# First addition of a layer's terms by an accumulating transfer, the last pairs' layer 2 apart, and quarter sums taken in an earlier sweep

## Chip, cores and metric

One core of one Trainium2 chip. The metric is device time in microseconds (us), the median of repeated executions of one program; lower is better. One further execution of the same program was taken with the hardware profiler.

## What is computed

Eight batches of a graph with 2048 nodes and 64 features go through four layers, each `x = layernorm(x + layer(x))`, all in fp32:

```python
# layer 0: Chebyshev terms of the adjacency A, weights made per node from an embedding of 16
As = [I, A, 2 A A - I]
x_g = einsum('knm,bmc->bnkc', As, x)
w   = einsum('nd,dkio->nkio', embedding, weight)
y   = einsum('bnki,nkio->bno', x_g, w) + einsum('nd,do->no', embedding, bias)
# layer 1: attention; e[i,j] = leaky_relu(s1[i] + s2[j]), masked by A > 0.5, softmax over j
y   = elu(einsum('bij,bjc->bic', softmax(where(A > 0.5, e, -9e15)), x))
# layer 2: (A + I) @ (x W^T + b) / rowsum(A + I)
# layer 3: node 0 set to given values, then three times
effects = einsum('nm,bmd->bnd', A, v)
v = relu([v, effects] @ W1^T + b1) @ W2^T + b2
```

A is 2048 x 2048, 16 MB, and does not stay on the chip: every product with it streams it again from device memory.

## The kernel before

Two batches make a pair, 128 columns, so there are four pairs (0 to 3). A product with A is a sweep: A comes as 32 tiles of 256 rows by 512 columns (512 KB each), and each tile feeds two fp32 matmuls of 128x512 per product (line 1094). Six buffers (`a_ring`) hold A tiles, and SyncE's queue (SP) fetches them in order (`fetch`, line 234). A sweep can serve two products from the same tiles.

Layer 0 needs two products with A for each pair. The first sweep serves pairs 0 and 1 (and also makes the layer 1 masks); the second product of a pair shares a sweep with the first product of a later pair, and the second product of pair 3 has a sweep of its own. After the two products come the per-node weights (`second_pass`, line 576): for each of 16 row tiles of a pair, 16 terms of 128x128 are made, one for each embedding element. PE makes eight at a time in `yp` (line 601), and `add_terms` (line 613) lets ScalarE (ACT) scale them by the embedding into a `terms` buffer of 1 MB, one of four in `e_ring` (line 624). For pairs 1 to 3 all 16 terms are stored; for pair 0 VectorE (DVE) folds the second eight onto the first eight (line 627), so eight are left. Line 636 then adds up the 16 (or 8) terms by one strided `tensor_reduce` into `added`, and line 639 adds `added` to the rows of the pair in `SX`.

Layer 1 (`layer1`, line 660) runs per pair and works mostly on DVE: `scores` finds each row's greatest score with 32 passes of 2048 elements (line 732), which need row masks loaded by GpSimd's queue (POOL, line 719); `weights` makes the softmax weights, with two additions on DVE (lines 810 and 823) and two kinds of activations on ACT (lines 818 and 826) for each of 32 column tiles, in buffers of the same `e_ring`, and PE multiplies them with the rows (line 837). `finish` normalises. A pair's rows are ready for layer 2 when `("x2", p)` is set.

Layers 2 and 3 of pairs 0 and 1 are one sweep and three sweeps each. Pairs 2 and 3 are joint (`JOINT`). Their layer 3 uses a Strassen-Winograd form: seven products of half size in place of eight, for which sums of the quarters of A are needed (`s1` to `s4`, 32 tiles in device memory). Before, `joint_layer2` (line 1189) makes layer 2 of both pairs in one sweep, which starts when both pairs are ready. It takes the tiles by groups of four, one of each quarter (`quarters`, line 1132), and after each group `sums` (line 1160) makes four sum tiles on DVE (line 1173), each in a buffer of `bc_ring`, and POOL's queue stores them (line 1175). Layer 2 reads A + I, so tiles on the diagonal are fetched again without I (`pure`, line 1150, eight in all).

The order is not left to a scheduler. A `Plan` (line 38) simulates the kernel while it is written: work is cut into generators ("threads"), each of which says which engine its next step needs and after what; `go` takes the step that can begin first, ties going to the lower rank, and adds a cost from small formulas (`dve`, `act`, `mm`, `plan.dma`). Instructions are emitted in that order, each engine executes its own in order, and semaphores keep the data safe. So a cost that is wrong in the plan does no harm to the values, but the engine then meets its instructions at other times than planned. A transfer is planned as 0.7 us of issue on POOL (0.4 on SP), 3.5 us, its size at 340 GB/s, and 0.2 us. `SLACK` (line 46) is added to the time at which PE may take a step.

Of the kernel before, what the change touches and what calls it, by code (L numbers as in the profile page):

```python
# [37 lines left out]
class Plan:  # L38
# [7 lines left out]
    SLACK = 1.0  # L46
# [97 lines left out]
def resnorm_d4_kernel(  # L144
# [288 lines left out]
    def row_tile(t, an, k, done):  # L433
        yield "ACT", [done]
        dg = tiny([P, 1], "dg", 2)
        nc.scalar.activation(an, an, AF.Copy, accum_out=dg)
        done = plan.run("ACT", act(N) + 0.2, done)
        yield "DVE", [done, mr_ring]
        nc.vector.tensor_scalar_add(dg, dg, 1.0)
        nc.vector.reciprocal(rdeg[:, t : t + 1], dg)  # L440
        mk, km = mr_ring.take([P, N], "mr", BF16)
        nc.vector.tensor_scalar(mk, an, THRESHOLD, NEG_INF, ALU.is_le, ALU.mult)
        done = plan.run("DVE", 1.13 + 0.26, done)
        bc_ring.give(k, done)
        nc.gpsimd.dma_start(by_row[t], mk)
        done = plan.dma("DMA", 512, done)
        mr_ring.give(km, done)
        at["by_row", t] = done
        if all(("by_row", i) in at for i in range(NT)):
            at["rows"] = done  # L450
# [99 lines left out]

    def stacks():

        for n in range(NPAIR * NCH):
            p, c = n // NCH, n % NCH
            yield "DMA", [xg_ring, ("y1T", p, c)]
            xg, kx = xg_ring.take([P, 2, CW], "xgT")
            nc.gpsimd.dma_start(
                xg[C:P], y1_cols[p].rearrange("(e c) n -> c e n", c=C)[:, :, cols(c)]
            )
            got = plan.dma("DMA", 256, xg_ring.t, ("y1T", p, c))  # L560
            yield "PE", [pp_ring]
            pt, km = pp_ring.take([P, CW], "ps_xg")
            for j in range(TPC):
                nc.tensor.transpose(pt[:, j * P : (j + 1) * P], SX[p][:, c * TPC + j, :], ident)
            t_pe = plan.run("PE", tr(TPC), pp_ring.t)
            for e in range(2):
                eng = yield EITHER, [t_pe]
                copy(eng, xg[0:C, e, :], pt[e * C : (e + 1) * C])
                done = plan.run(eng, cost(eng, CW), t_pe)
            pp_ring.give(km, done)  # L570
            stacked.append((xg, kx))
            at["xg", len(stacked)] = max(done, got)
# [40 lines left out]
    def add_terms(p, c, t, h, yp, ring, k, terms, t_pe, left):  # L613
# [16 lines left out]
        if h == 0:  # L630
            at["terms", p, t] = done
            return
        yield "DVE", [done]
        n = 8 if shared else D0
        added = tiny([P, P], "added", 1)
        nc.vector.tensor_reduce(  # L636
            added, terms[0][:, 0:n, :].rearrange("p d n -> p n d"), AX.X, ALU.add
        )
        nc.vector.tensor_tensor(v, v, added, ALU.add)
        done = plan.run("DVE", dve(n * P) + dve(P) + 0.1, done)  # L640
# [19 lines left out]
    def layer1(p):  # L660
# [7 lines left out]
        for c in range(NCH):  # L668
# [30 lines left out]
        plan.start(10 + p, scores(p, sv, xc, s_rows, done))  # L699

    def scores(p, sv, xc, s_rows, done):
        s2b = []
        for e in range(2):
            yield "DMA", [bc_ring, done, "rows"]
# [238 lines left out]
    def z_evict(p, c, pa, give, done):  # L943
# [4 lines left out]
        give(done)  # L948
# [187 lines left out]
    def order_of_joint():  # L1136
        for k in range(2):
            for r in range(RQ):
                order_of_a.extend((c, q, True) for c, q in quarters(k, r))
# [10 lines left out]
    def pure(k, r):  # L1150

        yield "SP", [("group", k, r), *([xg_ring] if len(xg_ring.freed) > 1 else [NEVER])]
        got = []
        for c, q in (quarters(k, r)[i] for i in (0, 3)):
            t, kt = xg_ring.take([P, 2, CW], "pure")
            nc.sync.dma_start(t, tile_of_adj(c, q))
            got.append((t, kt, plan.dma("SP", 512, xg_ring.t)))
        return got

    def sums(k, r, taken):  # L1160

        tiles4 = [(t, kt, got) for t, kt, got, _ in taken]
        own = {}
        if r // 2 == k:
            own = dict(zip((0, 3), (yield from pure(k, r))))
        a11, a12, a21, a22 = ((own.get(i) or tiles4[i])[0] for i in range(4))
        ready = [(own.get(i) or tiles4[i])[2] for i in range(4)]

        def out_of(m, a, b, op, *after):
            yield "DVE", [bc_ring, *after]  # L1170
            t, kt = bc_ring.take([P, 2, HALF], m)
            t = t.rearrange("p a b -> p (a b)")[:, 0 : 2 * CW].rearrange("p (t n) -> p t n", n=CW)
            nc.vector.tensor_tensor(t, a, b, op)
            done = plan.run("DVE", dve(2 * CW), *after)
            nc.gpsimd.dma_start(sum_tiles[m][k, r], t)  # L1175
            bc_ring.give(kt, plan.dma("DMA", 512, done))
            return t, done

        s3, d3 = yield from out_of("s3", a11, a21, ALU.subtract, ready[0], ready[2])
        s1, d1 = yield from out_of("s1", a21, a22, ALU.add, ready[2], ready[3])  # L1180
        s2, d2 = yield from out_of("s2", s1, a11, ALU.subtract, d1)
        s4, d4 = yield from out_of("s4", a12, s2, ALU.subtract, d2)
        for (_, kt, _, free), d in zip(taken, (d2, d4, d1, d1)):
            a_ring.give(kt, max(free, d))
        for _, kt, _ in own.values():
            xg_ring.give(kt, d2)
        refill()

    def joint_layer2():
        p, o = JOINT  # L1190
        at["group", 0, 0] = 0.0
        for k in range(2):
            pas = {}
            for r in range(RQ):
                taken = []
                for i, (c, q) in enumerate(quarters(k, r)):
                    n = next(used)
                    if r == 0 and i in (0, 2):
                        if i == 0:
                            yield "PE", [po_ring, ("x2", p), ("x2", o)]  # L1200
                            t2, kp = po_ring.take([P, 2, CW], "po")
                            pas[c] = [(t2[:, e, :], kp) for e in range(2)]
                        else:
                            pas[c] = []
                            for e in range(2):
                                yield "PE", [acc_ring]
                                pas[c].append(acc_ring.take([P, CW], "acc"))
                    for e, pair in enumerate(JOINT):
                        yield "PE", [("a", n)]
                        t, kt = a_tiles[n]  # L1210
                        for b in range(2):
                            m = 2 * q + b
                            nc.tensor.matmul(
                                pas[c][e][0],
                                lhsT=SX[pair][:, m, :],
                                rhs=t[:, b, :],
                                start=(r == 0 and i in (0, 2) and b == 0),
                                stop=(r == RQ - 1 and i in (1, 3) and b == 1),
                            )
                        done = plan.run("PE", mm(CW, 2), ("a", n))  # L1220
                        if r == RQ - 1 and i in (1, 3):
                            if i == 3:
                                give = lambda t, kk=pas[c][e][1]: acc_ring.give(kk, t)
                            else:
                                give = give_half(pas[c][e][1])
                            plan.start(1, z_evict(pair, c, pas[c][e][0], give, done))
                    del a_tiles[n]
                    taken.append((t, kt, at["a", n], done))
                    if i == 0:
                        nxt = (k, r + 1) if r + 1 < RQ else (k + 1, 0)  # L1230
                        at[("group", *nxt)] = plan.free["PE"]
                    spent[0] += 1
                plan.start(5, sums(k, r, taken))
                refill()

    halves_left = {}

    def give_half(kp):
        def give(t):
            left, last = halves_left.pop(kp, (2, 0.0))  # L1240
            if left == 1:
                po_ring.give(kp, max(t, last))
            else:
                halves_left[kp] = (1, max(t, last))

        return give
# [142 lines left out]
    def layer2_product(p):  # L1389
        return product(  # L1390
            SX[p],
            lambda c, pa, ka, done: z_evict(p, c, pa, lambda t: acc_ring.give(ka, t), done),
# [12 lines left out]
    def sweeps():  # L1405

        order_of_a.extend((c, q, False) for _ in range(NPAIR) for c, q in sweep_of_a)
        for p in range(NPAIR - 2):
            for s in range(4):
# [4 lines left out]
        for p in range(NPAIR):  # L1414
            products = [second_product(p)]
            if 0 < p < NPAIR - 1:
                products.append(first_product(p + 1))
            yield from sweep(*products)
        for p in range(NPAIR - 2):
            yield from sweep(layer2_product(p))  # L1420
            for s in range(3):
                yield from sweep(layer3_product(p, s))

# [3 lines left out]
        yield from joint_layer2()  # L1427
# [51 lines left out]
```

## Time and profile before

| | |
|---|---|
| runs shown | 2167.12, 2170.16, 2171.02 us; median 2170.16 |
| profiled execution | 2166.21 us; span in the trace 2164.4 us |
| mean granted TensorE clock | 0.991 |
| busy: PE, DVE, ACT, POOL | 2081.7, 1552.5, 977.9, 213.6 us |
| moved by the DMA engines | 495.84 MB, 229 GB/s over the span |

Where the stages lie, by the first and last instruction of their lines: the weights of layer 0 (line 601) from 149 to 1020 us; the sweep for pair 3's second product from 778 to 932 us; the layer 1 scores (line 732) from 332 to 1506 us and weights (line 810) from 423 to 1657 us; the joint layer 2 from 1675 to 1815 us, with its sums on DVE from 1692 to 1827 us; the joint layer 3 from 1815 to 2153 us.

How to read it: PE's rows are modelled at their end, so the distance from one start to the next, and the time in which PE has nothing begun, say more than the mean of a row. The page's slices are 54 us each. "A <- B" in a list of waits reads: the engine stood still before A, and B ended the wait. Waits of an engine off the path cost nothing by themselves. "PEld" is the loading of weights into PE; its idle time "<- issue" is its normal pace.

### The profile page before, as it was taken

Reading aid. Unit: us, or ns where it says so; the run is one execution under the profiler, and the core shown is the slowest. Engines: PE = TensorE matmul, PEld = TensorE weight load, DVE = VectorE, ACT = ScalarE, POOL = GpSimd, SP = SyncE. Lnnn points to the kernel's source line nnn. Section 1 sums busy time; section 2 is a strip of 40 time slices with the busy share of each in tenths; the row PEclk is TensorE's granted clock in tenths of the full one; section 3 lists DMA queues with packets and bytes.
Section 4 is the critical chain, followed back from the end, with each engine's and each line's share of the span. In section 5 each row is a group of like instructions: output and inputs, shape, how many; then the busy total and the mean of one; then the engine's idle time right before and its main releaser. Section 6 shows DMA issues by size and latency. Waiting matters only on the chain.

```text
span 2164.4 us, 18851 instructions
## 1 busy us (share of the span) xinstructions
PE 2081.7 (96%) x6325; PEld 917.0 (42%) x6325; DVE 1552.5 (72%) x1727; ACT 977.9 (45%) x1799; POOL 213.6 (10%) x374
## 2 busy tenths in 40 slices
PE   8999999899999999999999999999999899999998
PEld 3444344334333343333444454443444344444444
DVE  2227648998899999879999979999697455020214
ACT  0025424367776556767653757516676022000002
POOL 2310000101010110110001011010010110000000
PEclk9999999999999999999999999999999999999999
DMA  9899835634353364543669778788776667878785
GB/s 300 268 335 345 290 105 197 218 102 127 90 170 125 116 211 160 180 156 122 232 239 371 232 250 323 250 320 300 247 252 234 231 249 271 283 249 283 252 290 187
DMA packets 208739, 495.84 MB, mean 229 GB/s; under 512 B 20275, under 2 KB 28595, under 8 KB 204531
## 3 DMA queue, kind: packets, MB, share of 16 engines
q1 hardware_dynamic: 165058, 347.62, 47.2%
q0 software_dynamic: 39360, 144.92, 19.6%
q10 hardware_dynamic: 4224, 2.10, 0.4%
q8 instruction: 50, 0.82, 0.1%
q14 instruction: 47, 0.38, 0.1%
HBM read 446.14 MB, written 46.33 MB: 228 GB/s over the span
## 4 chain that ended last, share of the span: by engine, by line
PE 40%; DVE 26%; issue 25%; ACT 5%; DMA 3%; POOL 1%; POOLq 0%; ACTq 0%; SPq 0%; DVEq 0%
PE acc L1094 26%; DVE added L636 8%; PE po L837 6%; DVE junk L732 5%; DVE e L810 5%; PE yp L601 5%; DVE e L823 4%; ACT terms L624 2%; DMA a<-in_adj_t 2%; ACT e L818 1%; PE ps_u L1029 1%; PE acc L1083 1%; POOL s L1175 1%; ACT e L826 1%; DVE ln_v L495 1%
## 5 line engine op out<-in xcount | busy, mean ns | idle before, releaser
L1094 PE MATMUL acc<-a,SX 128*128 128x512 f32 x1024 | 467.3, 600 | 10.9 <-DMA SX<-in_x 6.6
L1094 PE MATMUL acc<-a,SA 128*128 128x512 f32 x768 | 352.5, 600 | 6.9 <-DMA a<-in_adj_t 6.2
L818 ACT ACTIVATE e<-e,sv 128x1024 f32<-128x1024 f32 x256 | 279.5, 1147 | 162.8 <-DVE e L810 161.6
L823 DVE TENSOR_TENSOR e<-e,mb 128x2048 f32<-128x2048 f32 x128 | 290.7, 2284 | 12.7 <-ACT e L818 12.0
L1094 PEld LDWEIGHTS acc<-a,SX 128*128 128x128 f32 x1024 | 191.5, 192 | 253.4 <-issue 237.7
L732 DVE CUSTOM_DVE_ANT_0 junk<-s2b,mr 128x2048 bf16<-128x2048 f32 x128 | 292.5, 2285 | 1.8 <-DMA mr<-by_row 0.5
L810 DVE TENSOR_TENSOR e<-s1b,mk 128x2048 f32<-128x2048 f32 x128 | 289.3, 2283 | 0.9 <-DMA mk<-by_col 0.6
L826 ACT ACTIVATE e<-e 128x2048 f32<-128x2048 f32 x128 | 245.1, 1919 | 92.8 <-DVE e L823 92.4
L624 ACT ACTIVATE terms<-yp,emb_sb 128x128 f32<-128x128 f32 x896 | 242.2, 394 | 78.5 <-PE yp L601 78.3
L601 PE MATMUL yp<-SH,xgT 128*128 128x512 f32 x512 | 248.9, 611 | 7.2 <-ACT terms L624 3.6
L636 DVE TENSOR_REDUCE added<-terms 128x128 f32<-128x2048 f32 (+1 forms) x64 | 208.0, 3249 | 47.7 <-ACT terms L624 47.5
L837 PE MATMUL po<-e,SX 128*64 128x512 f32 x1024 | 235.9, 602 | 2.2 <-ACT e L826 2.2
L1094 PEld LDWEIGHTS acc<-a,SA 128*128 128x128 f32 x768 | 141.1, 191 | 177.7 <-issue 166.1
L1300 PE MATMUL acc<-a,t 128*128 128x512 f32 x384 | 168.7, 592 | 0.0
L601 PEld LDWEIGHTS yp<-SH,xgT 128*128 128x128 f32 x512 | 91.3, 190 | 150.2 <-issue 133.6
L601 PE MATMUL yp<-SH,y2T 64*128 64x512 f32 x512 | 131.1, 626 | 7.8 <-ACT y2T L543 6.1
L837 PEld LDWEIGHTS po<-e,SX 128*64 128x64 f32 x1024 | 67.9, 137 | 152.2 <-issue 136.0
L805 POOL DMA_DIRECT2D mk<-by_col x128 | 69.2, 542 | 612.0 <-DVE e L810 576.1
L1094 PE MATMUL acc<-a,SB 128*128 128x512 f32 x256 | 120.7, 601 | 0.0
L1300 PEld LDWEIGHTS acc<-a,t 128*128 128x128 f32 x384 | 72.0, 190 | 86.1 <-issue 86.1
L601 PEld LDWEIGHTS yp<-SH,y2T 64*128 64x128 f32 x512 | 43.7, 188 | 88.3 <-issue 73.4
L491 ACT ACTIVATE ln_sq<-SX 128x512 f32<-128x512 f32 x48 | 30.4, 633 | 96.8 <-DVE SX L484 45.1
(225 smaller groups left out, 1676.0 us busy)
## 6 DMA issues: line engine op xcount, KB each, us to landing
a<-in_adj_t SPq DMA_DIRECT2D x496, 512.0 KB, 5.5
a<-s SPq DMA_DIRECT2D x96, 512.0 KB, 4.5
mr<-by_row POOLq DMA_DIRECT2D x64, 512.0 KB, 5.7
mk<-by_col POOLq DMA_DIRECT2D x128, 256.0 KB, 5.3
an<-in_adj SPq DMA_DIRECT2D x16, 1024.0 KB, 10.6
s<-s POOLq DMA_DIRECT2D x32, 512.0 KB, 5.2
a<-a_plus_i SPq DMA_DIRECT2D x24, 512.0 KB, 5.5
by_col<-mk POOLq DMA_DIRECT2D x32, 256.0 KB, 5.9
```

The source lines that it names most:

```text
L601: nc.tensor.matmul(yp[:, e, :], lhsT=y2T[rows, cs] if k2 else xg[:, e, cs], rhs=(wk2 if k2 else w01)[rows, hs], start=(k2 == h), stop=(k2 ...
L624: nc.scalar.activation(batches(terms[0][:, dd, :]), term, AF.Copy, scale=weight)
L636: nc.vector.tensor_reduce(added, terms[0][:, 0:n, :].rearrange("p d n -> p n d"), AX.X, ALU.add)
L732: nc.vector.tensor_tensor_reduce(out=junk, in0=s2b[e][0], in1=masks[t][0], scale=1.0, scalar=LOWEST, op0=ALU.add, op1=ALU.max, accum_out=m ...
L805: nc.gpsimd.dma_start(mk, by_col[jt // 2][:, jt % 2, h * HALF : (h + 1) * HALF])
L810: nc.vector.tensor_tensor(e, s1b[0], mk.unsqueeze(1).to_broadcast([P, 2, HALF]), ALU.add)
L818: nc.scalar.activation(e[:, i, :], e[:, i, :], AF.Prelu, bias=sv[:, 2 + i, jt : jt + 1], alpha=ALPHA)
L823: nc.vector.tensor_tensor(e, e, mb[0], ALU.add)
L826: nc.scalar.activation(e, e, AF.Exp)
L837: nc.tensor.matmul(po[i * C : (i + 1) * C, f, :], lhsT=SX[p][:, t, i * C : (i + 1) * C], rhs=e[:, i, f * CW : (f + 1) * CW], start=(t == 0 ...
L1094: nc.tensor.matmul(pa, lhsT=source[:, m, :], rhs=t[:, i, :], start=(m == 0 and not seed), stop=(m == NT - 1),)
L1300: nc.tensor.matmul(pa, lhsT=B[:, 2 * r + b, :], rhs=at_[:, b, :], start=(r == 0 and b == 0 and not go_on), stop=(r == RQ - 1 and b == 1), ...
```

## The change

Five things are edited.

1. In `add_terms`, for pairs 1 to 3, POOL's queue issues an accumulating transfer that adds terms 8 to 15 to terms 0 to 7, both in SBUF. DVE then adds four to four (512 elements), two to two (256), and each of the last two to the rows in `SX` (128 each). Pair 0, which has eight terms, takes the DVE steps alone. The strided reduction and `added` are gone.
2. Layer 2 of pairs 2 and 3 becomes two ordinary sweeps, one for each pair; `joint_layer2`, `pure` and `give_half` are gone.
3. The quarter sums move to the sweep of pair 3's second product in layer 0 (`sweep_with_sums`), which reads A without I. That sweep takes the tiles by groups of four quarters. DVE writes each sum over one of the four A tiles, and the tile's buffer is given back when POOL's store of it has landed. Pair 3's column chunks come in the order 0, 2, 1, 3.
4. Scores no longer wait for all the row masks (`"rows"`), only for the mask they read.
5. Constants of the planner: `SLACK` from 1.0 to 0.5; the rank of `scores` from 10 + p to 1.2 for pair 0 and 9.5 + p for the others; DVE's step after the terms is planned at 1.75 us.

```diff
-    SLACK = 1.0
+    SLACK = 0.5
...
-        if all(("by_row", i) in at for i in range(NT)):
-            at["rows"] = done
...
+    SUMS = 3
+    chunks_of = {p: (0, 2, 1, 3) if p == SUMS else (0, 1, 2, 3) for p in range(NPAIR)}
...
+        by_dma = not shared
+        if by_dma:
+
+            yield "DMA", [done]
+            nc.gpsimd.dma_start(terms[0][:, 0:8, :], terms[0][:, 8:16, :], accum_op=ALU.add)
+            done = plan.dma("DMA", 1024, done) + 1.0
         yield "DVE", [done]
-        n = 8 if shared else D0
-        added = tiny([P, P], "added", 1)
-        nc.vector.tensor_reduce(
-            added, terms[0][:, 0:n, :].rearrange("p d n -> p n d"), AX.X, ALU.add
-        )
-        nc.vector.tensor_tensor(v, v, added, ALU.add)
-        done = plan.run("DVE", dve(n * P) + dve(P) + 0.1, done)
+        for half in (4, 2):
+            a, b = (terms[0][:, i * half : (i + 1) * half, :] for i in range(2))
+            nc.vector.tensor_tensor(a, a, b, ALU.add)
+        for d in range(2):
+            nc.vector.tensor_tensor(v, v, terms[0][:, d, :], ALU.add)
+        done = plan.run("DVE", 1.75, done)
...
-        plan.start(10 + p, scores(p, sv, xc, s_rows, done))
+        plan.start(1.2 if p == 0 else 9.5 + p, scores(p, sv, xc, s_rows, done))
...
-            yield "DMA", [bc_ring, done, "rows"]
+            yield "DMA", [bc_ring, done]
...
+    def sweep_with_sums(source, evict, need):
+
         for k in range(2):
             pas = {}
             for r in range(RQ):
+                group = []
                 for i, (c, q) in enumerate(quarters(k, r)):
                     n = next(used)
                     if r == 0 and i in (0, 2):
+                        yield "PE", [acc_ring]
+                        pas[c] = acc_ring.take([P, CW], "acc")
+                    yield "PE", [("a", n), *need(q // 2)]
+                    t, kt = a_tiles.pop(n)
+                    for b in range(2):
+                        nc.tensor.matmul(
...
+                    group.append((t, kt, done))
                     spent[0] += 1
+                    if i == 3:
+                        plan.start(0, sums(k, r, group))
+                    refill()
+
+    def sums(k, r, group):
+
+        (a11, _, d11), (a12, _, d12), (a21, _, d21), (a22, _, d22) = group
+        for i, m, out, a, b, op, after in (
+            (3, "s1", a22, a21, a22, ALU.add, (d21, d22)),
+            (2, "s3", a21, a11, a21, ALU.subtract, (d11, d21)),
+            (0, "s2", a11, a22, a11, ALU.subtract, (d11,)),
+            (1, "s4", a12, a12, a11, ALU.subtract, (d12,)),
+        ):
+            yield "DVE", after
+            nc.vector.tensor_tensor(out, a, b, op)
+            done = plan.run("DVE", dve(2 * CW) + 0.03, *after)
+            nc.gpsimd.dma_start(sum_tiles[m][k, r], out)
+            a_ring.give(group[i][1], plan.dma("DMA", 512, done))
+        refill()
...
+        by_quarters = [t for k in range(2) for r in range(RQ) for t in quarters(k, r)]
+        for p in range(NPAIR):
+            order_of_a.extend((c, q, False) for c, q in (by_quarters if p == SUMS else sweep_of_a))
...
             products = [second_product(p)]
+            if p == SUMS:
+                yield from sweep_with_sums(*second_product(p)[0:3])
+                continue
...
+        yield from sweep(layer2_product(NPAIR - 2))
...
-        yield from joint_layer2()
+        yield from sweep(layer2_product(NPAIR - 1))
         yield from joint_layer3()
```

## The prediction, made before the result

> **What bounds the kernel now.** I read the page's busy totals and 40 slices first, then busy time by stage, then what the matmul engine waited for in the stage with most idle time, then the costliest groups, then the transfers.
>
> ```profile
> PE 2081.7 (96%) x6325; PEld 917.0 (42%) x6325; DVE 1552.5 (72%) x1727; ACT 977.9 (45%) x1799; POOL 213.6 (10%) x374
> ...
> PE   8999999899999999999999999999999899999998
> ...
> DVE  2227648998899999879999979999697455020214
> ```
>
> PE is full nearly everywhere, and VectorE (DVE) is full too from slice 7 to slice 30 (about 330 to 1660 us). So the end is set by PE's work plus PE's idle time, and DVE can only matter by making PE idle. The stages (columns: stage, length, then busy time of PE, PEld, DVE, ACT, POOL, then clock, DMA share, GB/s):
>
> ```profile
> 0.00:400.00 400.00, 386.23 (x1071) 169.94 (x1073) 214.44 (x392) 124.93 (x339) 57.53 (x95) 0.99 0.75 256
> 400.00:1050.00 650.00, 616.99 (x1885) 247.66 (x1883) 603.80 (x501) 433.16 (x946) 63.90 (x116) 0.98 0.47 153
> 1050.00:1660.00 610.00, 599.36 (x1987) 267.07 (x1984) 568.51 (x544) 357.19 (x381) 67.00 (x121) 1.00 0.78 271
> 1660.00:1850.00 190.00, 174.78 (x543) 86.52 (x542) 91.89 (x164) 33.84 (x75) 19.10 (x35) 0.98 0.71 253
> 1850.00:2164.00 314.00, 304.33 (x845) 145.84 (x843) 73.86 (x129) 28.81 (x59) 6.04 (x8) 0.99 0.77 257
> ```
>
> Length minus PE busy is PE idle: 13.8, 33.0, 10.6, 15.2 and 9.7 us, 82 in all. That is the whole prize. In the stage with 33 us, PE's own waits are (what waited, for whom: total, times, longest):
>
> ```profile
> PE ps_xg L564 <- ACT terms L624: 7.0, 2, 4.2
> PE ps_rows L785 <- DVE mx L755: 6.6, 2, 4.7
> PE yp L601 <- ACT y2T L543: 6.1, 1, 6.1
> PE yp L601 <- ACT terms L624: 3.9, 4, 2.0
> PE ps_rows L785 <- ACT terms L624: 3.3, 1, 3.3
> ```
>
> All are DVE, or ScalarE (ACT) work that itself stood behind DVE: over the run ACT's line 818 waited 161.6 us for DVE's line 810. None waits for a transfer. DVE is 93% busy here, and the group below is a quarter of it (155 of 604 us):
>
> ```profile
> L636 DVE TENSOR_REDUCE added<-terms 128x128 f32<-128x2048 f32 x48 | 177.3, 3694 | 47.5 <-ACT terms L624 47.5
> L636 DVE TENSOR_REDUCE added<-terms 128x128 f32<-128x1024 f32 x16 | 30.7, 1916 | 0.2
> L639 DVE TENSOR_TENSOR SX<-SX,added 128x128 f32<-128x128 f32 x64 | 18.7, 292 | 2.2
> ```
>
> The planner in the code counts 2.2 us for such a reduction. It took 3.69, so DVE fell 1.5 us per tile behind the order written for it, and PE, which runs in that order, met the lateness.
>
> **What the skill says.** "Perfetto Trace Analysis", Identifying the Most-Contended Engine, warns that matmul busy time is a poor measure because matmuls are pipelined. I therefore use idle time; the 512-column matmul instructions follow each other every 0.43 us where nothing waits, though their rows say 600 ns. "DMA: Bandwidth & Descriptors", SWDGE vs HWDGE vs iDMA: an accumulating transfer can only be issued from GpSimd, so the new ones join POOL's queue; the trace of before has none. "SBUF — State Buffer", Who interferes with whom: a two-input tensor_tensor contends with GpSimd's reads, and descriptor generation is thought to need the write side. The trace agrees: mk loads issued beside line 810's tensor_tensor take 542 ns, mr loads beside the scoring 535. The tree should not slow POOL. Price: "VectorE: DVE Perf Modes", The TRN2 errata: fp32 tensor_tensor is (N+151)/0.96 ns; the trace has 292 at 128, 687 at 512, 1220 at 1024, so I use it for 256 (424 ns).
>
> **The change part by part.** The instruction order of the kernel as built shows 3299 PE matmuls before and after, so PE's work stays and I only move its idle time. Changes of PE between kinds of work are as many as before (some 250 each), worth nothing.
>
> *Reduction to tree.* Before, a tile holds DVE 3.74 us from the reduction's start to the addition's, and 0.21 to the next instruction: 3.95. After: 0.69 + 0.42 + 2 x 0.29 with three dependent steps of about 0.03 and the same overlap at the end: 1.71. Saved: 48 x 2.24 = 107 us, and 16 x 0.45 = 7 for pair 0, together about 115 us. 42 of the 48 lie in the 400-1050 stage: 94 us off its 604. The planner now counts 1.75, so its order no longer drifts (48 x 1.5 = 72 us of drift gone).
>
> *Accumulating transfers.* 48, each adding 512 KB of SBUF to 512 KB of SBUF. On POOL's queue they cost 48 x 0.54 = 26 us of issue, beside a POOL that is 10% busy. Queued behind each, while it waits for ACT's last term, are mask loads (who waits: line 810 on DVE), score loads and the sum stores. The landing time is not in the trace. From below: the DMA page's Anatomy section gives 2.0 us + bytes/436 GB/s = 3.2 us, an estimate from that page (POOL's plain 512 KB rows land in 5.2 to 6.4, so it is too low here). From above: it reads both operands, and POOL's 1 MB rows land in 8.2 to 10.1 us; with a loaded queue 12. I take 8. The tree is placed 7.7 us after issue (3.5 + 3.0 + 0.2 + 1.0 in the planner), so at 8 it costs about nothing; 3.2 gains nothing, as the order is fixed; 12 is the rival below. The terms buffer is held longer by those 8 us less 2, with four buffers shared with the layer 1 weights: a little, in the 3 us below.
>
> *Sums.* 32 tensor_tensors of 1.22 us = 39 us of DVE go from the 1660-1850 stage to the sweep of pair 3 in layer 0, that is into the full stage. Its DVE load becomes 604 - 94 + 39 = 549. The 32 stores (17 MB) move too. They write over the A tiles, and the SP queue's next fetches wait for the stores: about 1.2 + 0.5 + 5.2 us, then a fetch of 5.5, some 13 us a group of four tiles. In the built order each group has 10 to 15 us of other PE work behind it, which hides it; without that cover it is 8 x 13 = 104 us.
>
> *Layer 2 of pairs 2 and 3 apart.* Pair 2's sweep (64 matmuls of 0.86 = 55 us) now stands before pair 3's rows are needed. The wait for them (4.2 us, line 1213 on DVE SX), the tile wait behind the extra loads (2.9) and most of the transposes' 5.1 us go: about 10 of the 15.2. What is late next is pair 2's own normalisation, under pair 3's sweep. A tiles: 32 more fetches and 8 "pure" fewer, net 12.6 MB on SP.
>
> *Order knobs* (less slack, no wait for all mask rows, pair 0's scores earlier): bounded at 3 us either way, taken as nothing. Pair 3's scoring now asks 370 GB/s for about 110 us; the full stretch at 1150-1180 us moved 384, so the 10.6 us there stays.
>
> Sum of PE idle: 13.8 stays; 33.0 becomes 8 (a quarter kept, since DVE at 549 still fills 88% of the stage) plus 3 for new waits; 10.6 stays; 15.2 becomes 5; 9.7 stays. That is 50, against 82: minus 32 us. The profiled execution took 2166.2 (span 2164.4), 4 under the median of 2170.2; so 2134 for a profiled one, and **2138** for the median.
>
> **The rivals.** *Slower: the accumulate lands late.* DVE runs in order, so a tree whose transfer isn't there stops the layer 1 work behind it, and ACT and PE with it. After the change the stage has 46 + 94 - 39 = 101 us of free DVE time, 2.4 us for each of its 42 tiles. Beyond 7.7 + 2.4 = 10.1 us of landing, each us costs up to 42. The gain of 32 is used up at about 11 us. At 12 us it is 1.9 x 42 = 80, halved because many trees start late anyway: 2138 + 40 = **2178**. For it: 1 MB rows reach 10.1. Against: the DMA share is 0.47 in this stage.
>
> *A held A ring.* Six buffers, four in a group's hands: if the cover falls short by 2.5 us a group, 8 x 2.5 = 20 us come back: **2158**. For it: SP's fetches are in order, so one late store stops all. Against: the built order has work there.
>
> *The relief changes nothing.* The waits re-form behind ACT or behind PE's fixed order: **2170**. For it: DVE at 88% is still nearly full. Against: the waits listed all lead back to DVE.
>
> **How the numbers follow.** Forecast 2138 (2122 to 2152): 0.50. Below 2122, where all 48 us of the two stages go: 0.06. Held ring 2158: 0.20. No change: 0.07. Late accumulate 2178: 0.17. About 0.2% (4.3 us) is what a measurement of this kernel can tell from no change: faster 0.50 + 0.06 + 0.20 = 0.76, same 0.07, slower 0.17. The range goes from 2112 (all idle of the two stages and most tile waits gone: 2170 - 48 - 8 = 2114) to 2176, just short of the slower rival.
>
> **What would show it.** Right: PE idle near 11 us in the layer 0 and 1 stage and near 5 around layer 2 of the last pairs; no reduction row, trees of about 1.7 us; accumulates landing under 9 us; DVE 70 us to 115 us less busy. Wrong: DVE waiting on the terms transfer for more than 30 us in all; PE waiting for A tiles inside the pair 3 sweep; PE waiting for ACT terms as before though DVE has time.

## Result, and the profile after

The changed kernel takes 2164.28 us (median of 20 runs, 2157.38 to 2168.45), beside 2167.57 us for the kernel before on the same chip. The ratio is 0.9982, 95% interval 0.9973 to 0.9991: 3 us faster, where 32 were forecast. The profiled execution took 2167.19 us (span 2165.4).

VectorE (DVE) did lose its work. These are the busy totals, the 40 slices and the granted clock of the page after:

```profile
PE 2087.1 (96%) x6325; PEld 921.1 (43%) x6325; DVE 1438.9 (66%) x1855; ACT 988.0 (46%) x1799; POOL 257.6 (12%) x422
...
PE   8999999999999998999698999999999999999997
...
DVE  2227546997789998769998989999796322120214
...
PEclk9999999999999998999899999999999999999999
```

DVE is 113.6 us less busy (forecast 115). PE shows a hole in slice 19 (1028 to 1083 us), where its clock falls as well; the kernel before had none there. The busy times in the forecast's five stages of the kernel after (columns as before):

```profile
0.00:400.00 400.00, 383.59 (x1058) 169.44 (x1059) 193.02 (x425) 123.15 (x331) 66.00 (x105) 0.98 0.79 265
400.00:1050.00 650.00, 629.00 (x1899) 254.29 (x1899) 559.48 (x631) 443.62 (x952) 118.17 (x189) 0.98 0.71 216
1050.00:1660.00 610.00, 580.95 (x1932) 255.25 (x1929) 554.28 (x530) 356.19 (x374) 65.13 (x118) 0.98 0.74 257
1660.00:1850.00 190.00, 190.00 (x598) 96.69 (x597) 57.89 (x142) 36.17 (x85) 2.29 (x3) 1.00 0.79 265
1850.00:2165.00 315.00, 303.59 (x843) 145.46 (x841) 74.27 (x129) 28.92 (x59) 6.02 (x8) 0.99 0.76 255
```

PE idle is 16.4, 21.0, 29.0, 0 and 11.4 us; the forecast had 13.8, 11, 10.6, 5 and 9.7. The stage around layer 2 of the last pairs did better than forecast, and the one after layer 0, which was to stay, has 18 us more. PE's longest waits in that stage:

```profile
PE po L843 <- ACT e L832: 8.8, 3, 5.9
PE ps_vT L1022 <- DVE v L1014: 8.3, 1, 8.3
PE acc L1100 <- DMA a<-in_adj_t: 5.9, 6, 2.9
PE ps_emb L988 <- DVE SB L997: 2.7, 2, 2.1
```

`ps_emb` (line 988) and `ps_vT` (line 1022) are the tails of pair 0's layer 2. PE's instructions there, as the timeline has them (start, duration, line, operation, count, and the idle time before):

```profile
1067.70 2.05 PE L988 MATMUL ps_emb<-w2bd,z 128*128 128x128 f32 x16
1071.84 1.13 PE L988 MATMUL ps_emb<-w2bd,z 128*128 128x128 f32 x8 [2.09 <-DVE SB L997]
1073.60 1.13 PE L988 MATMUL ps_emb<-w2bd,z 128*128 128x128 f32 x8 [0.64 <-DVE SB L997]
1083.05 0.48 PE L1022 MATMUL ps_vT<-ident,v 128*128 128x128 f32 x1 [8.33 <-DVE v L1014]
1083.32 0.85 PE L1022 MATMUL ps_vT<-ident,SB 128*128 128x128 f32 x3
1084.10 5.55 PE L843 MATMUL po<-e,SX 128*64 128x512 f32 x16
```

PE waits 8.33 us for a chain of dependent normalisation steps on DVE and ACT, with nothing else to do. In the kernel before, the first `ps_emb` came at 1044.4 us, while pair 0's layer 2 sweep began its last matmul at 1065.5 and covered the chain. After, the sweep began its last matmul at 1055.9 and the first `ps_emb` came at 1067.7. What holds it is the first line of `tails` (line 979 of the kernel after): `yield "PE", [("x1", NPAIR - 1)]`. No tail may begin before pair 3's rows have left layer 0, since the tails write the rows that layer 3 starts from into `SH`, where the weights of layer 0 (`w01`, `wk2`) still lie. The last product of layer 0 (`yp`) ended at 1020.1 us before and at 1036.6 after. I call this wait the gate. The stretch 1020 to 1125 us, first of the kernel before, then of the kernel after:

```profile
1020.00:1125.00 105.00, 102.50 (x360) 46.13 (x359) 104.08 (x103) 66.92 (x87) 8.03 (x15) 1.00 0.66 221
```

```profile
1020.00:1125.00 105.00, 85.12 (x299) 37.41 (x298) 100.47 (x109) 61.56 (x81) 8.26 (x15) 0.92 0.55 183
```

PE idle goes from 2.5 to 19.9 us, and the mean clock from 1.00 to 0.92: another 105 x 0.08 = 8.4 us lost while PE is busy. The trace's record of the clock shows what that is: the clock is granted at 0.5 for 3.4, 6.8, 10.2 or 13.7 us at a time, mostly behind a wait, and 512-column matmuls then follow each other every 0.853 us instead of 0.43.

So PE loses time in two ways, and I count both. Waits: the distance from the start of one PE instruction to the next, beyond 0.53 us for 512 columns and 0.13 for fewer (twice that at half clock). Half clock: half of the time in which the record says 0.5, up to PE's last matmul, counted in the stage in which the stretch begins.

| stage (us) | before: waits + half clock | after | difference |
|---|---|---|---|
| 0 to 400 | 10.6 + 3.4 | 13.4 + 6.8 | +6.2 |
| 400 to 700 | 17.7 + 5.1 | 5.6 + 3.4 | -13.8 |
| 700 to 1020 | 16.3 + 5.1 | 14.5 + 8.5 | +1.6 |
| 1020 to 1125 (gate) | 3.4 + 0 | 21.1 + 8.5 | +26.2 |
| 1125 to 1660 | 11.6 + 0 | 14.2 + 3.4 | +6.0 |
| 1660 to the end | 19.2 + 3.4 | 1.7 + 0 | -20.9 |
| sum | 78.9 + 17.1 | 70.5 + 30.7 | +5.3 |

The span minus this sum is 2060 to 2070 us in all kernels below but 13 and 14, so differences of the sum give differences of the time to within some 10 us. Gains of 35 us in two stages are there; the gate takes 26 back, and the other three stages 14.

### The profile page after: what moved, and what is told of

It is laid out like the page before. It is cut to its first block, busy times and chain, and to the rows that moved or that the text cites. A ratio compares the mean times of both kernels' runs of the same rounds, so it can differ in the third digit from the quotient of the medians.

```text
span 2165.4 us, 19202 instructions
## 1 busy us (share of the span) xinstructions
PE 2087.1 (96%) x6325; PEld 921.1 (43%) x6325; DVE 1438.9 (66%) x1855; ACT 988.0 (46%) x1799; POOL 257.6 (12%) x422
## 4 chain that ended last, share of the span: by engine, by line
PE 55%; issue 26%; DVE 9%; DMA 6%; ACT 2%; POOL 1%; SPq 0%; POOLq 0%; DVEq 0%; ACTq 0%
PE acc L1100 30%; PE yp L602 11%; PE po L843 9%; DMA a<-in_adj_t 3%; DVE junk L738 3%; DVE e L816 2%; DVE e L829 1%; DVE a L1193 1%; PE ps_u L1035 1%; ACT terms L625 1%; DMA an<-in_adj 1%; PE acc L1089 1%; ACT e L824 1%; PE pf L877 1%; DVE terms L643 1%
## 5 line engine op out<-in xcount | busy, mean ns | idle before, releaser
L1100 PE MATMUL acc<-a,SX 128*128 128x512 f32 x1280 | 580.7, 598 | 9.5 <-DMA SX<-in_x 6.6
L1100 PEld LDWEIGHTS acc<-a,SX 128*128 128x128 f32 x1280 | 238.3, 192 | 296.7 <-issue 283.9
L829 DVE TENSOR_TENSOR e<-e,mb 128x2048 f32<-128x2048 f32 x128 | 290.4, 2287 | 17.9 <-ACT e L824 17.1
L843 PE MATMUL po<-e,SX 128*64 128x512 f32 x1024 | 241.3, 613 | 15.9 <-ACT e L832 15.8
L643 DVE TENSOR_TENSOR terms<-terms 128x512 f32<-128x512 f32 (+1 forms) x128 | 71.1, 556 | 43.7 <-DMA terms<-terms 41.1
L489 ACT ACTIVATE ln_sq<-SX 128x512 f32<-128x512 f32 x48 | 30.7, 640 | 115.4 <-DVE SX L1001 44.5
L1073 POOL DMA_DIRECT2D out<-SX x12 | 9.1, 756 | 517.9 <-DVE SX L508 517.9
```

The source lines that it names most:

```text
L643: nc.vector.tensor_tensor(a, a, b, ALU.add)
L829: nc.vector.tensor_tensor(e, e, mb[0], ALU.add)
L843: nc.tensor.matmul(po[i * C : (i + 1) * C, f, :], lhsT=SX[p][:, t, i * C : (i + 1) * C], rhs=e[:, i, f * CW : (f + 1) * CW], start=(t == 0 ...
L1100: nc.tensor.matmul(pa, lhsT=source[:, m, :], rhs=t[:, i, :], start=(m == 0 and not seed), stop=(m == NT - 1),)
```

## Experiments

All kernels compute the whole reference. "End of layer 0" is when the last `yp` ended; "loss" is waits plus half clock, in all and "at the gate", by which the table means the whole stretch from 1020 to 1125 us. Layer 0 ends outside that stretch in 13 and 14. Times are medians of 4 runs, of 12 in kernels 9 and 12, and of 20 in 3, 7 and the changed kernel; each ratio is to the kernel before on the same chip.

| run | us | ratio to before, 95% | end of layer 0 | loss in all | at the gate |
|---|---|---|---|---|---|
| before | 2167.57 | | 1020.1 | 96.0 | 3.4 |
| changed | 2164.28 | 0.9982 (0.9973 to 0.9991) | 1036.6 | 101.2 | 29.6 |
| 1 tree and transfer alone | 2188.11 | 1.0088 (1.0071 to 1.0104) | 1067.4 | 124.3 | 49.5 |
| 2 changed, reduction back | 2202.61 | 1.0159 (1.0139 to 1.0179) | 1079.7 | 139.6 | 29.0 |
| 3 changed, SLACK back | 2172.1 | 1.0022 (1.0013 to 1.003) | 1044.2 | 107.1 | 31.6 |
| 4 changed, scores back | 2145.72 | 0.9893 (0.9872 to 0.9914) | 1014.3 | 77.0 | 18.8 |
| 5 changed, gate moved | 2142.26 | 0.9885 (0.9868 to 0.9902) | 1034.4 | 72.5 | 2.6 |
| 6 as 4, gate moved | 2147.02 | 0.9895 (0.9854 to 0.9936) | 1020.9 | 74.4 | 2.1 |
| 7 as 1, gate moved | 2162.98 | 0.9981 (0.9974 to 0.9988) | 1067.7 | 96.2 | 26.1 |
| 8 tree on DVE alone | 2140.11 | 0.9874 (0.9857 to 0.9891) | 1013.6 | 65.9 | 9.2 |
| 9 as 8, tree planned late | 2168.2 | 1.0002 (0.9991 to 1.0013) | 1044.9 | 106.1 | 33.2 |
| 10 changed, tree on DVE | 2142.97 | 0.9885 (0.9869 to 0.99) | 1025.3 | 73.1 | 2.1 |
| 11 as 10, gate moved | 2144.95 | 0.9898 (0.9881 to 0.9915) | 1023.2 | 74.3 | 0.7 |
| 12 before, true cost planned | 2169.41 | 1.001 (0.9999 to 1.0021) | 994.4 | 107.9 | 14.1 |
| 13 as 1, hold not planned | 2317.57 | 1.0698 (1.0682 to 1.0714) | 1186.9 | 273.7 | |
| 14 changed, hold not planned | 2303.93 | 1.0638 (1.0621 to 1.0656) | 1167.8 | 261.6 | |
| 15 as 10, scores back | 2157.21 | 0.9953 (0.9936 to 0.9969) | 1042.9 | 95.7 | 19.2 |
| 16 sums and layer 2 alone | 2183.11 | 1.0076 (1.0059 to 1.0094) | 1055.1 | 118.2 | 4.2 |
| 17 as 8, gate moved | 2131.65 | 0.984 (0.9824 to 0.9857) | 1014.0 | 63.8 | 0.6 |

The theories I began with: A, the moved sums ate the gain. B, the amount of DVE work does not set PE's idle time; each new fixed order brings waits of its own, and the half clock after them. C, the transfers cost what the tree saves. D, the planner's smaller SLACK costs; D2, the scores' new place in the order costs.

### 1 to 4: parts alone, parts undone

**1.** The kernel before with edit 1 alone:

```diff
+            nc.gpsimd.dma_start(terms[0][:, 0:8, :], terms[0][:, 8:16, :], accum_op=ALU.add)
+            done = plan.dma("DMA", 1024, done) + 1.0
...
-        nc.vector.tensor_reduce(
+        for half in (4, 2):
```

> The kernel before with the accumulating transfer and the tree alone: sums stay in the joint layer 2, the planner's knobs stay. DVE falls by about 115 us against before. Theory A (the sums moved into the full stage ate the gain): this run keeps the gain, near 2140 us, with about 10 us of PE idle time less per 400 us in layers 0 and 1. Theory B (the amount of DVE work does not set PE's idle time; each new fixed order brings its own local waits, and a halved PE clock after them): within 10 us of before, 2158 to 2178, although DVE is 110 us less busy.

2188.11, slower than before by 21 us. A falls, since without the moved sums nothing is gained. The time lies above B's range too. Layer 0 ended at 1067 us and the gate lost 49.5 us.

**2.** The changed kernel with the reduction, its old cost in the plan, and no transfer:

```diff
-            nc.gpsimd.dma_start(terms[0][:, 0:8, :], terms[0][:, 8:16, :], accum_op=ALU.add)
...
+        nc.vector.tensor_reduce(
```

> The changed kernel with the old strided reduction and its old planned cost back (no accumulating transfer, no tree). DVE rises by about 115 us. If the relief of DVE was worth what I forecast and another part of the change ate it, this run is 20 to 40 us slower than the changed kernel, 2185 to 2205. Theory B: between 2160 and 2185, the loss coming from a few waits of PE for DVE. Theory C (the accumulating transfers cost what the tree saves): equal to the changed kernel, 2160 to 2168, with the waits of DVE for terms (41 us) gone.

2202.61, in the first of the expected ranges: inside the change the tree with its transfer is worth 38 us, but alone it costs 21. C falls in its simple form, and the parts do not add up.

**3.**

```diff
-    SLACK = 0.5
+    SLACK = 1.0
```

> The changed kernel with the planner's slack back at 1.0. Theory D (half the slack lets PE meet its instructions too early, and that ate the gain): 15 to 30 us faster than the changed kernel, 2135 to 2150. Theory B: a different order with different waits, within 10 us either way, 2154 to 2174.

2172.1, 8 us worse. D falls.

**4.**

```diff
-        plan.start(1.2 if p == 0 else 9.5 + p, scores(p, sv, xc, s_rows, done))
+        plan.start(10 + p, scores(p, sv, xc, s_rows, done))
...
-            yield "DMA", [bc_ring, done]
+            yield "DMA", [bc_ring, done, "rows"]
```

> The changed kernel with the scores' ranks (10 + p) and their wait for all row masks as before. Theory D2 (starting the scores earlier put DVE work where PE then waits for it): 10 to 25 us faster than the changed kernel. Theory B: within 10 us either way, 2154 to 2174.

2145.72, 18.6 us better, and layer 0 ends 22 us earlier. D2 holds in this kernel. Of the 24 us of loss that go, 11 lie in the stretch of the gate and 13 elsewhere.

The four times do not follow DVE's work, and in 1 and in the changed kernel the gate has the largest new loss. That made the next theory, G: the loss is the gate's, when layer 0 ends late.

### 5 to 7 and 17: the gate moved

The tails need only that the last product of layer 0 has read its weights, not that the rows are normalised:

```diff
             xg_ring.give(kx, t_pe)
+            if n == NPAIR * NCH - 1:
+                at["w0_read"] = t_pe
...
-        yield "PE", [("x1", NPAIR - 1)]
+        yield "PE", ["w0_read"]
```

The same edit was put into the changed kernel (5) and into kernels 4, 1 and 8 (6, 7 and 17).

> The changed kernel, with one wait moved: the tails of layer 2 (the matmuls with the embedding that bring the weights of layer 3) wait until the last matmul of layer 0 has read its weights, and no longer until pair 3's rows of layer 0 are normalised. Theory G (gate: in the changed kernel layer 0 of pair 3 ends 17 us later and layer 1 is ahead, so that pair 0's layer 2 sweep ends before its tails may begin and PE has nothing else; of the 101 us of PE waits and half clock, 30 lie in 1020 to 1125 us against 3 in the kernel before): these 30 shrink to some 10, and the time falls by 12 to 22 us to 2142 to 2152. Theory B (each new fixed order brings its own waits elsewhere, and this one's place is chance): the waits re-form, 2154 to 2174, within 10 us of the changed kernel either way.

2142.26: G holds. Layer 0 ends at 1034.4, as late as in the changed kernel, yet the stretch of the gate is full again:

```profile
1020.00:1125.00 105.00, 103.10 (x364) 46.40 (x363) 102.05 (x112) 65.56 (x85) 8.41 (x15) 1.00 0.73 235
```

Of the loss of 29.6 us there 2.6 are left, no other stage gained more than 1, and the time fell by 22 us.

> The kernel of the fourth experiment (changed kernel with the scores' rank and their wait for all mask rows back, 2145.7 us) with the same wait moved. Theory G: it still had 19 us of waits and half clock in 1020 to 1125 us, of which 8 to 14 go: 2132 to 2138, at which the forecast would have been met. Theory B: 2140 to 2152.

2147.02: missed. Its four runs spread from 2134 to 2151. The gate lost almost nothing any more (2.1), but waits came back before and after it, as B had it. So scores back (4), the gate moved (5) and both (6) give about the same time, and the gains do not add. They are not one loss all the same: kernel 4 still waited 7.4 us for `ps_vT` at the gate, and more than half of what it saved lay elsewhere.

> The kernel before with the accumulating transfer and the tree alone (2188.1 us), with the same wait moved. Theory G: it had 50 us of waits and half clock in 1020 to 1125 us, of which 20 to 40 go: 2148 to 2168, below the kernel before. Theory B: 2178 to 2198.

2162.98: 25 us better, as G had it. The tails now run between the parts of pair 0's sweep, and the two long waits that kernel 1 had behind their steps on DVE (8.9 and 5.4 us) are gone; the longest that is left behind the tails is 1.7. What stays of the 26 us in this stretch is no matter of the gate: mainly, before layer 0 ends at 1067 us, PE waits 12.5 us in three places for the exponentials of layer 1 (12.4 in kernel 1), with half clock behind.

> The kernel of the eighth experiment (tree on DVE alone, 2140.1 us, 9 us of waits and half clock in 1020 to 1125 us) with the tails' wait moved as in the fifth. If the gate costs on its own: 2130 to 2136. If the waits come back elsewhere: 2137 to 2148.

2131.65, the fastest kernel here, 35 us below the kernel before on the same chip, and in the first of the two ranges. Its profiled execution, the slowest of its four, shows less: the 9 us at the gate went to 0.6, but the loss in all only from 65.9 to 63.8.

### 8 to 11: what makes layer 0 late

Theory H: the transfer's time, during which a `terms` buffer (four in all, shared with layer 1's weights) is not free.

**8.** The kernel before with a tree wholly on DVE and no transfer:

```diff
-        nc.vector.tensor_reduce(
+        for half in (4, 2) if shared else (8, 4, 2):
...
+        done = plan.run("DVE", 1.75 if shared else 2.9, done)
```

> The kernel before with the reduction replaced by a tree that is wholly on DVE (eight to eight, four to four, two to two, then two additions to the rows; planned at 2.9 us), without the accumulating transfer. Theory H (the terms buffer, held some 7 us longer for the transfer, is what pushes the end of layer 0 of pair 3 back, from 1020 to 1067 us in the kernel with tree and transfer): without the transfer the last product of layer 0 ends before 1045 us and the time is below that kernel's 2188, some 2160 to 2172, though DVE has 1.2 us a tile more to do. Against H (any shorter step for DVE lets the planner put layer 1 ahead of layer 0): the last product ends after 1050 us, and the time is 2178 to 2200.

2140.11: H, and 20 us better than it asked. DVE is busy 1495.3 us, 56 more than in the changed kernel, and the time is 24 us less.

**9.** The same kernel, the tree planned as if a transfer stood before it:

```diff
+        if not shared:
+            done += 7.7
         yield "DVE", [done]
```

> The kernel of the eighth experiment (kernel before with a tree wholly on DVE, 2140.1 us) with one edit to the plan: DVE may take the tree of pairs 1 to 3 only 7.7 us after the last term, as if a transfer stood between. There is no transfer, and the same work. Theory H1 (what costs in tree and transfer alone is that a terms buffer is held some 8 us longer in the plan, so that the planner finds other work for PE and layer 0 of pair 3 ends late): last product of layer 0 after 1045 us and a time of 2165 to 2190. Theory H2 (the cost is the transfers on the chip, 41 us of DVE's waits in the changed kernel, and the place on POOL's queue): last product before 1025 us and 2136 to 2150.

2168.2: 28 us slower with the same instructions in another order, and layer 0 ends at 1044.9 instead of 1013.6. H1 asked for more than 1045 us and a time from 2165. The edit delays both the tree and the release of its buffer; which of the two moves the order is not shown. The same two waits are back at the gate:

```profile
PE po L838 <- ACT e L827: 10.4, 3, 7.3
PE ps_vT L1017 <- DVE v L1009: 8.3, 1, 8.3
```

**10.** The changed kernel with the tree of 8:

```diff
-            nc.gpsimd.dma_start(terms[0][:, 0:8, :], terms[0][:, 8:16, :], accum_op=ALU.add)
...
-        for half in (4, 2):
+        for half in (4, 2) if shared else (8, 4, 2):
```

> The changed kernel with its tree wholly on DVE (planned at 2.9 us), without the accumulating transfer; all else as changed. If the transfer's longer hold of the terms buffer is what ate the gain, the last product of layer 0 comes before the changed kernel's 1036.6 us, and the time is 2120 to 2145. If the scores' place in the order and the moved sums ate it, 2155 to 2170, as the changed kernel.

2142.97: without the transfer 21 us come back, and the gate loses 2.1 us. But in 700 to 1020 us the sweep with sums (line 1161 here) now waits for A tiles:

```profile
PE acc L1161 <- DMA a<-in_adj_t: 12.2, 6, 4.3
```

In the changed kernel this is 0.4. That stage loses 26.7 us in all, against 1.3 in kernel 8: more than the 11 us by which the sums and the separate layer 2 shorten the end, and 10 is no better than 8.

**11.** Kernel 10 with the edit of 5.

> The kernel of the tenth experiment with the tails' wait moved as in the fifth. If both causes are one (a late end of layer 0 that shows at the tails), this is within 6 us of the tenth experiment where that one has under 10 us of waits in 1020 to 1125 us. If they are two, it is 8 to 20 us below it. In either case 2115 to 2140.

2144.95, within 2 us of 10: in this kernel transfer and gate are one loss, as the first case of the expectation had it; the time is 5 us over its range. It is also within 3 us of 5, so once the gate is moved, the changed kernel is no slower with the transfer than without.

### 12 to 16: plan and chip

**12.** The kernel before, its reduction planned at what it takes:

```diff
-        done = plan.run("DVE", dve(n * P) + dve(P) + 0.1, done)
+        done = plan.run("DVE", 2.15 if shared else 3.95, done)
```

> The kernel before, its reduction unchanged, but planned at what it takes (3.95 us, and 2.15 for pair 0, in place of 2.4 and 1.3). No instruction is added or removed. The forecast held that the kernel before loses because its order drifts by 1.5 us a tile from the plan. If that is so, a plan with the true cost is 8 to 20 us faster: 2148 to 2160. If the tree gains by the 57 us of DVE work that it saves and not by the plan, this is 2164 to 2180.

2169.41: the wrong cost in the plan was not what the kernel before lost by. The waits in 400 to 700 us do go (17.7 to 1.4), and come back after 1125 us (11.6 to 26.4, with 10.2 of half clock).

**13** and **14.** Kernel 1 and the changed kernel, the transfer kept, its time taken out of the plan:

```diff
-            done = plan.dma("DMA", 1024, done) + 1.0
+            plan.dma("DMA", 1024, done)
+            done += 0.5
```

> The kernel before with the accumulating transfer and the tree alone (2188.1 us), with one edit to the plan: the tree is planned 0.5 us after the transfer's issue instead of after its landing (some 7.7 us). The transfer and the tree stay. If the 48 us against the tree on DVE are the hold in the plan, the last product of layer 0 comes before 1035 us and the time is 2135 to 2155. If they are the transfer on the chip, DVE now stands at the tree until it lands, about 5 us for each of 48 tiles of which the slack takes some, and the time is 2165 to 2200.

> The changed kernel with the same edit to the plan. If the hold in the plan is what ate the gain, 2130 to 2150 and a last product of layer 0 before 1030 us. If the transfers on the chip do, DVE's wait for them grows from 41 us to over 150 us in all and the time is 2160 to 2190.

2317.57 and 2303.93. My own guess of 2135 to 2155 was far off, and so was the other bound. DVE now stands before nearly every tree (kernel 13; total, times, longest):

```profile
DVE terms L643 <- DMA terms<-terms: 283.0, 46, 27.2
```

The transfer takes 6.0 us here, no longer than elsewhere; what stands behind it on DVE is layer 1, and with it ACT and PE, which lose 192 us in waits and 82 at half clock. So in these kernels the time in the plan cannot simply be left out: it costs 28 us by the order that it forces (9), and leaving it out costs 130 to 140. A reserve between 0.5 and 7.7 us, such as the measured 6 us, was not tried. Leaving the time out does not take the order and the transfer apart.

**15.** Kernel 10 with the edit of 4.

> The kernel of the tenth experiment with the scores' rank and their wait for all mask rows back. If the early scores take PE's other work away from the sweep with sums, PE's wait for A tiles in 700 to 1020 us falls from 12 us to under 5 and the time is 2120 to 2136. If that wait comes from the stores of the sums themselves, it stays at 8 us or more, and the time is 2138 to 2150.

2157.21, outside both expectations: PE's wait for A tiles in the sweep grew to 15.0 us, and the gate, with layer 0 ending at 1042.9, costs 19 us again. The same edit that gained 18.6 us in 4 loses 14 here. Why the planner ends layer 0 later in this case I did not settle.

**16.** The kernel before with the sums in layer 0 and layer 2 of the last pairs apart (edits 2 and 3), all else as before:

```diff
+            if p == SUMS:
+                yield from sweep_with_sums(*second_product(p)[0:3])
+                continue
...
+        yield from sweep(layer2_product(NPAIR - 2))
...
-        yield from joint_layer2()
+        yield from sweep(layer2_product(NPAIR - 1))
```

> The kernel before with only the quarter sums in the sweep of pair 3's layer 0 and layer 2 of pairs 2 and 3 apart (reduction, SLACK, ranks and the wait for all mask rows as before). By the forecast's steps 10 of the 15 us of idle time around the joint layer 2 go and the sums are hidden: 2155 to 2162. If the sums in the full stage delay the end of layer 0 (the store and fetch of A tiles, and 39 us more of DVE), waits and half clock rise by 10 us or more in 700 to 1125 us: 2165 to 2190.

2183.11, slower by 16.5. From 1660 us on 21 us are gained, but in 700 to 1020 us waits and half clock go from 21 to 59 us. PE waits there for ACT, whose work stands behind DVE's, not for tiles (700 to 1125 us):

```profile
PE po L840 <- ACT e L829: 24.7, 6, 9.8
...
PE acc L1164 <- DMA a<-in_adj_t: 0.7, 1, 0.7
```

With the reduction still there, DVE has no room for 39 us of sums: in 700 to 1020 us it was busy 294.8 of the 320 us before, and is busy 303.1 here. The changed kernel, with the tree, loses 23 in that stage. The tree's gain lies partly here: it pays for the sums.

## Why the prediction was wrong

The time lies in the range (2112 to 2176) and 26 us above the forecast of 2138. That it lies in the range is no support for the sum: PE idle, forecast at 50 us, came to 77.8, of which 18.4 too much lie in the stage that was to stay and 10 in the stage 400 to 1050. The steps, in turn:

- **Reduction to tree**: right. 113.6 us less DVE work, and the waits in 400 to 700 us fell by 13.8 us with half clock. The clause that the order "no longer drifts" explained nothing: the plan with true costs (12) gains nothing. Less DVE work did not carry through to the end where the transfer came with it (1). Without the transfer it did: kernel 8, with 57 us less DVE work than the kernel before, is 27 us faster, and its loss in 400 to 1020 us falls from 44.2 to 16.1, which is where the forecast expected the relief to pay.
- **Accumulating transfers**: the step that failed. I priced their landing (8 us, measured 6.1 in the median, 4.5 to 15.8) and their issue (26 us, measured 42: 0.88 each, not 0.54), and took the longer hold of a buffer as "a little, in the 3 us below". The rows of the kernel after:

```profile
L643 DVE TENSOR_TENSOR terms<-terms 128x512 f32<-128x512 f32 (+1 forms) x128 | 71.1, 556 | 43.7 <-DMA terms<-terms 41.1
...
terms<-terms POOLq DMA_DIRECT2D x48, 512.0 KB, 6.1
```

  By this count DVE waits 41.1 us for them in six places, over the 30 us that I had named as a sign of being wrong. But 26.6 of them are one wait that ended at 338 us with a transfer issued only at 332.5, so at most 5.7 us of it belong to the transfer. The price is in the plan: 28 us for the planned latency alone (9 against 8), and 21 in the changed kernel (10), where it falls on the gate. I had compared 7.7 us with the landing, and not asked what the planner does with PE in those 7.7 us. What runs late next is pair 3's layer 0, and behind it the gate. "10.6 stays" was the term that this upset: 29.0.
- **Order knobs**: "taken as nothing, bounded at 3 us" was wrong too. The scores' place is worth 18.6 us here (4), SLACK 8 the other way (3).
- **Sums**: hidden, as said (PE waits 0.4 us for tiles in that sweep), but only together with the tree. Alone they cost 37 us in their stage (16). The DVE load there came to 559 us (forecast 549, which is 84% of the 650 us, not the 88% it gave).
- **Layer 2 apart**: right in kind, too small. The stage of 15.2 us went to 0, not 5.
- **POOL undisturbed by the tree**: not tested by the figures that I gave. The loads of 542 ns and those of 535 both ran beside DVE instructions that read two tensors (lines 810 and 732).
- **PE idle as the whole prize**: one term was missing. The half clock after waits cost 17.1 us before and 30.7 after, 13.6 more, a part of the 29 us of gain that did not come; idle time does not show it.

Of the rivals, the late accumulate has its mechanism shown in 13 and 14, but with the wait planned it didn't come. The held A ring shows in 10 and 15 (12 to 15 us), not in the changed kernel. "The relief changes nothing" came near the time by another way: the waits behind DVE in 400 to 700 us did go, and others took their place at a barrier I had not looked at. Taking that barrier away brings the changed kernel to 2142.26, within 4 us of the forecast (5).

What stays open: why 6, 7, 15 and the change itself differ in the order that the planner finds. Each is one greedy order, and differences of 5 to 10 us between them have no cause shown here. Nor is it shown how much of the gain of kernel 8 is the relief of DVE and how much its order.

## What to carry to other kernels

Where a planner fixes the order, a latency that is planned costs by the order it forces, even if the engine never waits for it: price it by asking which buffers it holds and what is late at the next barrier. Before you count on freed engine time, list the barriers behind the stage and the slack of each; here one wait, stricter than its data needed, was worth 22 us. With that wait relaxed and no other part of the change made, a tree wholly on DVE (17, 2131.65) beats the tree with a transfer (7, 2162.98), though it leaves DVE 55 us busier; inside the whole change the two come out alike (11 and 5).

## What the runs showed of the hardware

A stall of PE can cost more than its length. In the 19 profiles, of the waits (counted as above) that began at full clock, all 84 of 4 us or more are followed, within 1 us of their end or while they last, by a stretch at 0.5 of the clock; within 9 us the same holds for 56 of the 72 from 2.5 to 4 us and 22 of the 48 from 2 to 2.5. The shortest single wait behind which such a stretch stands is 1.41 us; in one place two waits of 0.87 and 0.82 us stand before it. Not every stretch has a wait: in 15 of the 19 profiles one begins between 76 and 81 us, at or just behind a row of 32 matmuls of 16x64, with no wait above 0.08 us before it. The stretches last 3.4 us or multiples of it. The Trainium skill ("TensorE: Matmul & The Clock Gate", HAM oscillation) gives "no PE-idle gaps >~3.4µs" as the rule; the unit agrees, but here stretches also follow gaps well below it. In the kernel after, 13.7 us at half clock lie on a chain of small matmuls at 845 to 863 us, with four waits in it, one of 1.46 us and three of 0.73.

An accumulating transfer of 512 KB within SBUF held POOL's queue for 0.88 us at issue (0.85 to 0.95), where plain loads took 0.54 to 0.58, and landed in 6.1 us, as a plain row load did (6.9).
